# Window and rotary attention with feed-forward on one core: row-strip products split into 32-column squares, part of the first softmaxes moved to ScalarE

## The chip, the cores and the metric

The kernel runs on one NeuronCore of a Trainium2 chip. The time is device time in microseconds (us), taken over whole executions; a separate execution was recorded by the hardware profiler. TensorE (PE) multiplies into PSUM, VectorE (DVE), ScalarE (ACT) and GpSimd (POOL) do the elementwise work, SyncE (SP) issues most transfers.

## What is computed

Sixteen sequences of 512 tokens with 256 channels pass through four blocks, each added to its input:

```python
x = x + window_attention(layernorm(x))   # stage a
x = x + ffn(layernorm(x))                # stage f
x = x + rotary_attention(layernorm(x))   # stage b
x = x + ffn(layernorm(x))                # stage h, same weights as f
```

All is float32. Both attentions have 16 heads of 16 channels. Stage a is a softmax over a window of 32 keys to each side and the first 4 keys; the first 4 queries see all keys. Stage b divides exponentials of rotated scores by the sum of exponentials of unrotated ones, and masks causally after that:

```python
num = exp(q_rot @ k_rot.T * scale)
den = exp(q @ k.T * scale).sum(-1, keepdims=True)
y = where(causal, num / den, 0) @ v
ffn(x) = (silu(x @ wg.T) * (x @ wu.T)) @ wd.T      # 256 -> 768 -> 256, integer weights times 1/127
```

## The kernel before

One program holds all 16 sequences. A planner inside the kernel (`Plan`, from L85) writes out the order of every engine's instructions by hand. Each piece of work is an `Op` (L57) with an engine, an estimated duration, names that it needs, slots that it takes and gives, and for TensorE a "lying": how the 128 x 128 array is divided.

- `ROWS`: four strips of 32 rows. A head pair holds 32 channels of the contraction, so four head pairs are multiplied side by side, each into its own PSUM bank. `nm` (L1219, rotated scores) and `dn` (L1153, unrotated scores) take 128 weight columns, `sa` (L730, window scores) takes 64, with the two halves of a tile of 128 queries beside each other.
- `COLS`: four strips of 32 columns, with all 128 rows: the products of weights with values (`ya` L894, `yb` L1279) and, when the neighbours lie so, the projections (`product`, L440).
- `FULL`: the whole array: transposes (`tp` L838, `lt` L503, `tg` L964, `pgp` L866) and projections. `FLEX` work takes `FULL` after `FULL` and `COLS` otherwise.

The planner picks among the ready ops of an engine. For TensorE it adds to an op's progress an amount from `TURN` where the array would have to be divided anew, keeps row work together for `TURN["hold"]`, and counts `BORDER` for a change. `LEAD` and `SHARE` say how far the stages of one sequence run apart; all four stages of neighbouring sequences are interleaved. These numbers order the work; they are not measured times.

Stage a of a sequence projects keys, queries and values, then for each of four tiles of 128 queries computes `sa` into four banks, adds the mask into a score buffer `sc` (two of them) and runs a softmax over two halves of the heads: maximum on VectorE (L773), subtraction on POOL (L775), one exponential over 1056 columns on ScalarE (L782), sum and reciprocal on VectorE (L784, L785), scaling on POOL (L790). Then `tp` transposes the weights four heads at a time, and the results `pt` are copied out of PSUM, alternately by VectorE (L843) and ScalarE (L845). Stage b runs 16 `dn` groups of four products of 512 columns, each followed by four exponentials with a running sum on ScalarE (L1134), and 10 `nm` groups in whose causal part the columns are 512, 384 + 128 or 256 + 256, each followed by four exponentials (L1185) and a causal selection on POOL (L1195).

The first two sequences' stage a stands alone at the start, since nothing else is ready. The buffer `ht` holds the integers of `wd` until they are scaled, and later the hidden layer of a feed-forward.

Of the kernel before, what the change touches and what calls it, by code (L numbers as in the profile page):

```python
# [15 lines left out]
P = 128  # L16
S = 512
# [39 lines left out]
class Op:  # L57
# [1 line left out]


    def __init__(
        self, engine, us, *needs, takes=(), gives=(), makes=None, lying=FULL, sbuf=False
    ):
        self.engine, self.us, self.needs = engine, us, needs
        self.takes, self.gives, self.makes, self.lying = takes, gives, makes, lying
        self.sbuf = sbuf
        self.end, self.k = 0.0, {}

def pe(us, *needs, **how):
# [9 lines left out]
    return Op("pool", us or 0.15 + 0.0017 * n, *needs, **how)  # L79

LAG = {"pe": 0.26, "act": 0.2, "dve": 0.2, "pool": 0.2, "sp": 0.1}
BORDER = 0.19
NEVER = 1e9

class Plan:  # L85
# [68 lines left out]
    def run(self):  # L154
        while True:
            self.threads = [t for t in self.threads if t[1] is not None]
            if not self.threads:
                return
            cand = []
            for t in self.threads:  # L160
                op = t[1]
                at = self.ready(op)
                if at >= NEVER:
                    continue
                start = max(at, self.free[op.engine])
                if op.engine == "pe" and at > self.free["pe"]:
                    start += 0.1
                if op.sbuf:
                    start = max(start, self.sbuf)
                cand.append((start, t))  # L170
            assert cand, [(t[2], t[3], t[1].needs, t[1].takes) for t in self.threads]
            least, t = min(cand, key=lambda c: c[0])
            engine = t[1].engine
            soon = [
                c
                for c in cand
                if c[1][1].engine == engine
                and c[0]
                <= least + (TURN["hold"] if engine == "pe" and self.lying == ROWS == c[1][1].lying else 0.05)
            ]  # L180
            if engine == "pe":
                start, t = min(
                    soon,
                    key=lambda c: (
                        c[1][4],
                        self.progress(c[1]) + self.turn(c[1][1]),
                    ),
                )
            else:
                start, t = min(soon, key=lambda c: (not c[1][1].gives, c[1][4], self.progress(c[1])))  # L190
            op = t[1]
            us = op.us
            if engine == "pe":
                op.lying = self.lies(op)
                if op.lying != self.lying:
                    us += BORDER
                self.lying = op.lying

                if start - self.free[engine] > 1.5:
                    self.slow = start + 4.2  # L200
                if start < self.slow:
                    us += min(us, (self.slow - start) / 2)
                key = t[2], t[3]
                self.done[key] = self.done.get(key, 0.0) + us
            if op.sbuf:
                self.sbuf = start + us
            self.take(op)
            self.free[engine] = start + us
            op.end = start + us + LAG[engine]
            self.give(op, op.end)  # L210
            if op.makes:
                self.at[op.makes] = op.end
            try:
                t[1] = t[0].send(op)
            except StopIteration:
                t[1] = None


TURN = {"hold": 0.35, "fr": 0.05, "fc": 0.3, "rf": 0.02, "cf": 1.0, "rc": 0.05, "cr": 0.1}
LEAD = {"a": 0.0, "f": 1.015, "b": 1.665, "h": 2.889}  # L220
SHARE = {"a": 44.0, "f": 33.0, "b": 66.0, "h": 33.0}

@with_exitstack
def kernel(
# [152 lines left out]
    def dequantized():  # L377

        for at, t, raw, by, name in (
            (15.0, wg_sb, raw_wg, DEQUANT, "wg"),  # L380
            (17.0, wu_sb, raw_wu, DEQUANT, "wu"),
            (19.0, wd_sb, raw_wd, 0.5 * DEQUANT, "wd"),
        ):
            yield dve(0, at, us=0.9, makes=name, sbuf=True)
            nc.vector.tensor_scalar(t, raw, by, None, ALU.mult)
        yield dve(0, 25.0, us=1.0, makes="sins", sbuf=True)
        nc.vector.tensor_reduce(sign, perm, AX.X, ALU.add, negate=True)
# [2 lines left out]
    def values_bias():  # L390
# [3 lines left out]
        for kc in range(NC):  # L394
# [27 lines left out]
            "va": 1,  # L422
            "vw": 1,
            "sg": 1,
            "small": 2,
            "pq": 2,
            "gs": 1,
            "yg": 1,
# [4 lines left out]
            "ht": 1,  # L433
        }
    )
    x_slot = {}
    xnt = {}
    before = {"f": "a", "b": "f", "h": "b"}
# [2 lines left out]
    def product(out, w, moving, lying, **how):  # L441

        strips = [slice(32 * j, 32 * j + 32) for j in range(4)] if lying == COLS else [slice(P)]
        for s in strips:
            nc.tensor.matmul(out[s], w[:, s], moving, skip_group_check=True, **how)  # L445

    def one(op, emit):
        emit((yield op))
# [158 lines left out]
    def window_attention(b):  # L607
# [62 lines left out]
        for oc in range(NC):  # L670
# [12 lines left out]
            takes=("u", "sg"),  # L683
            gives=[("tmp", q_slot[oc]) for oc in range(NC)],
            lying=FLEX,
        )
        sgp = bank(op, [P, NT, H * NG], f"sgp_{b}")
        for t in range(NT):
# [23 lines left out]
        for t in range(NT):  # L712
# [2 lines left out]
                f"qa_{me}.0",  # L715
                f"qa_{me}.1",
                f"scored_a{b - 1}",
                takes=("s", "sc", "small"),
                makes=f"scored_{me}" if t == NT - 1 else None,
                gives=[(lock, 0) for lock in locks] if t == NT - 1 else (),  # L720
                lying=ROWS,
# [2 lines left out]
            for oc in range(NC):  # L724
                for par in range(2):
                    for half in range(2):
                        for j in range(4):
                            rows = slice(32 * j, 32 * j + 32)
                            u = 2 * t + half
                            nc.tensor.matmul(  # L730
                                ps[j][U * half : U * half + U, oc, par, :],
                                tiles["qa"][rows, par, oc, u * U : (u + 1) * U],
                                keys[rows, oc, u * U : u * U + P],
                                start=True,
                                stop=True,
                            )
            go(softmax(b, t, op, ps, sg), -1 if t < 2 else 0)

    kept = {}

    def softmax(b, t, op, ps, sg):


        me = f"a{b}"
        mask = mask3[:, 0 if t == 0 else 2 if t == NT - 1 else 1, :]
        sc = buf(op, "sc", [P, 4, NC, 2, P + NG], f"sc_{b}_{t}")
        small = buf(op, "small", [P, 2, H], f"sm_{b}_{t}")
        flat = sc.rearrange("p j c two w -> p (j c two) w")
        kept[b, t] = sc, small, op.k["sc"], op.k["small"]
        k_s, at = op.k["s"], op.end  # L750
        op = yield dve(
            0, at, f"sg_{me}", us=0.17, gives=(("sg", 0),) if t == NT - 1 else (), sbuf=True
# [17 lines left out]
        def half(hs, start, name):  # L770
            part = flat[:, hs, :]
            op = yield dve(0, *start, us=1.17)
            nc.vector.tensor_reduce(small[:, 0, hs], part, AX.X, ALU.max, negate=True)  # L773
            op = yield pool(0, op.end, us=1.9, sbuf=True)
            nc.gpsimd.tensor_tensor(  # L775
                part,
                part,
                small[:, 0, hs].unsqueeze(2).to_broadcast([P, H // 2, P + NG]),
                ALU.add,
            )  # L780
            op = yield act(1056, op.end)
            nc.scalar.activation(part, part, AF.Exp, scale=SCALE)  # L782
            op = yield dve(0, op.end, us=1.17 + 0.15)
            nc.vector.tensor_reduce(small[:, 1, hs], part, AX.X, ALU.add)  # L784
            nc.vector.reciprocal(small[:, 1, hs], small[:, 1, hs])  # L785
            op = yield pool(0, op.end, us=1.9, makes=f"sc_{me}.{t}.{name}", sbuf=True)
            if name:
# [12 lines left out]
    def global_values(b, v_all):  # L800

        me = f"a{b}"
        op = yield pe(0.43, f"v_{me}.0", takes=("u",), lying=FLEX)
        vg_ps = bank(op, [P, S], f"vgp_{b}")
        product(
            vg_ps[:, :D], spread, v_all[:, 0, :, 0::2, :], op.lying, start=True, stop=True
# [6 lines left out]
    def weighted(b):  # L813
# [10 lines left out]
        def read(t):  # L824

            left[t] = left.get(t, len(parts) + 1) - 1
            return (("sc", kept[b, t][2]),) if left[t] == 0 else ()

        def turns():
            for t in range(NT):  # L830
                for n, (oc, par) in enumerate(parts):
# [5 lines left out]
                    for j in range(4):  # L837
                        nc.tensor.transpose(ps[:, j, :], sc[:, j, oc, par, 0:P], ident)  # L838

                    def keep(_, t=t, n=n, par=par, ps=ps, op=op):  # L840
                        pt = buf(op, "pt", [P, 4, P], f"pt_{b}_{t}_{n}")
                        if par:
                            nc.vector.tensor_copy(pt, ps)  # L843
                        else:
                            nc.scalar.copy(pt, ps)  # L845
                        pts[t, n] = pt, op.k["pt"]

                    how = dict(gives=(("u", op.k["u"]),), makes=f"pt_{me}.{t}.{n}")
                    go(one(dve(S, op.end, **how) if par else act(S, op.end, **how), keep), -1)

        def weights(t):

# [20 lines left out]
        for t in range(NT):  # L873
            go(weights(t))
            for ns in (range(4),):
                op = yield pe(
                    0.22 * len(ns),
                    *(f"pt_{me}.{t}.{n}" for n in ns),
                    f"vw_{me}",
                    takes=("u",) if 0 in ns else (),  # L880
# [51 lines left out]
    def global_queries(b, qg, keys, v_all, v_lock):  # L932

        me = f"a{b}"
        R = H * NG
        op = yield pe(0.9, takes=("u", "gs"), lying=COLS)
        ps = bank(op, [P, S], f"gq_{b}")
        for oc in range(NC):
            nc.tensor.matmul(
# [106 lines left out]
    def rotary_attention(b):  # L1046
# [91 lines left out]
        for oc in range(NC):  # L1138
            for par in range(2):
                for t in range(NT):  # L1140
# [9 lines left out]
                    ps = banks(op, [P, S], f"dn_{b}_{oc}_{par}_{t}")  # L1150
                    for j in range(4):
                        rows = slice(32 * j, 32 * j + 32)
                        nc.tensor.matmul(  # L1153
                            ps[j],
                            tiles["qb"][rows, par, oc, t * P : (t + 1) * P],
                            tiles["kt"][rows, oc, :],
                            start=True,
                            stop=True,
                        )
                    go(exponentials(oc, par, t, ps, op.k["s"], op.end, last))  # L1160

# [44 lines left out]
        for i, (oc, segments) in enumerate(groups):  # L1206
# [9 lines left out]
            for c, par, at in segments:  # L1216
                n = S - c * P
                for j, rows in enumerate(strips):
                    nc.tensor.matmul(  # L1219
                        ps[j][:, at : at + n],  # L1220
                        tiles["kr"][rows, oc, c * P : (c + 1) * P],
                        tiles["qr"][rows, par, oc, c * P :],
                        start=True,
                        stop=True,
                    )
            go(causal(i, segments, ps, op), -1)

# [31 lines left out]
    def products(b, groups, made, strips):  # L1259
        me = f"b{b}"  # L1260
        seen = set()
        for i, (oc, segments) in enumerate(groups):
            first = i % (len(groups) // NC) == 0
            last = (i + 1) % (len(groups) // NC) == 0
            op = yield pe(0.8, f"num_{me}.{i}", takes=("u",) if first else (), lying=COLS)
            if first:
                seen = set()
                k_u = op.k["u"]
# [178 lines left out]
```

## Time and profile before

| | us |
|---|---|
| median of 3 runs | 2588.65 (2588.26 to 2593.74) |
| profiled execution | 2590.7 |
| its span | 2589.0 |
| TensorE busy | 2531.6, 98% |
| VectorE, ScalarE, POOL busy | 1578.8, 1456.5, 949.7 |
| `dn`, one matmul record (2048, four at a time) | 0.636 |
| `nm`, one record of 512 columns (512) | 0.632 |
| `sa`, one record (4096, eight at a time) | 0.284 |

A float32 product is carried out in two passes, and each pass is one record of a weight load (PEld) and one of a matmul (PE); transposes take one pass. Records of strips that run side by side overlap, so a record's duration says little about throughput; the distance from one group's start to the next one's does. The mean granted clock of TensorE over the execution is 0.99 of full speed.

### The profile page before, as it was taken

To read this page: it belongs to the slowest core of one execution; us is meant where nothing else is said; L and a number is where in the kernel's file an instruction comes from. 1 tells how busy PE (TensorE), PEld (TensorE's weight loads), DVE (VectorE), ACT (ScalarE), POOL (GpSimd) and SP (SyncE) were. 2 spreads that over 40 slices of the span, in tenths; PEclk is the share of its full clock that TensorE was granted. 3 is DMA by queue.
4 is the path that set the end of the run, shared out by engine and by line. 5 is a ranking of instruction groups with operands and counts; after the bars stand their busy time and mean duration, and the time that the engine had idled before them with its cause. 6 is when DMAs were issued, how large, how long until landed. Compare 5 with 4: busy or idle time off the path is not lost.

```text
span 2589.0 us, 78357 instructions
## 1 busy us (share of the span) xinstructions
PE 2531.6 (98%) x34688; PEld 1286.3 (50%) x34688; DVE 1578.8 (61%) x3062; ACT 1456.5 (56%) x3553; POOL 949.7 (37%) x971
## 2 busy tenths in 40 slices
PE   7899999999999999999999999999999999999998
PEld 5454445454454544545455454544545455454444
DVE  7975748476583755847467484665837558374332
ACT  2356664745547465474755647465474754647473
POOL 5634425153251524425153250533515144151211
PEclk8999999999999999999999999999999999999999
DMA  4000010000101000010000100000010000100000
GB/s 140 26 25 2 2 41 2 25 18 10 33 2 28 15 25 18 2 41 2 25 18 2 41 2 25 19 21 21 2 34 9 25 18 2 33 2 1 10 9 9
DMA packets 26675, 50.76 MB, mean 20 GB/s; under 512 B 2336, under 2 KB 21216, under 8 KB 26336
## 3 DMA queue, kind: packets, MB, share of 16 engines
q1 hardware_dynamic: 24976, 44.83, 6.1%
q8 instruction: 272, 4.46, 0.7%
q10 hardware_dynamic: 1360, 0.93, 0.1%
q14 instruction: 67, 0.55, 0.1%
HBM read 13.77 MB, written 8.39 MB: 9 GB/s over the span
## 4 chain that ended last, share of the span: by engine, by line
PE 85%; DVE 12%; ACT 1%; DMA 1%; POOL 1%; issue 1%; POOLq 0%; DVEq 0%; ACTq 0%
PE dn L1153 9%; PE psc_uh L445 7%; PE psc_gh L445 7%; PE nm L1219 7%; PE po_h L445 7%; PE psc_gf L445 7%; PE psc_uf L445 6%; PE po_f L445 6%; PE yb L1279 5%; PE tp L838 3%; PE sa L730 3%; PE psv_a L445 2%; PE po_b L445 2%; PE psc_qa L445 2%; PE ya L894 2%; DVE tmpb L1064 2%
## 5 line engine op out<-in xcount | busy, mean ns | idle before, releaser
L1134 ACT ACTIVATE dn<-dn 128x512 f32<-128x512 f32 x1024 | 599.4, 585 | 121.0 <-PE dn L1153 118.0
L1185 ACT ACTIVATE ptb<-nm 128x512 f32<-128x512 f32 x640 | 328.8, 610 | 241.1 <-PE nm L1219 240.8
L1195 POOL TENSOR_SCALAR_AFFINE_SELECT ptb<-ptb 128x512 f32<-128x512 f32 x256 | 160.5, 637 | 537.0 <-ACT ptb L1185 521.1
L775 POOL TENSOR_TENSOR sc<-sc,sm 128x1056 f32<-128x1056 f32 x128 | 248.8, 1951 | 258.1 <-DVE sm L773 250.2
L1153 PE MATMUL dn<-kt,qb 32*128 32x512 f32 x2048 | 295.8, 636 | 0.4 <-DVE vb L572 0.4
L790 POOL TENSOR_TENSOR sc<-sc,sm 128x1056 f32<-128x1056 f32 x128 | 249.8, 1952 | 49.9 <-DVE sm L785 34.4
L445 PE MATMUL psc_uh<-xnt_h,wu_sb 128*32 128x512 f32 (+1 forms) x1164 | 184.4, 598 | 10.7 <-DVE pt L843 10.7
L1134 ACT ACTIVATION_READ_ACCUMULATOR dn<-dn 128x1 f32 x1024 | 192.0, 188 | 0.0
L445 PE MATMUL psc_gh<-xnt_h,wg_sb 128*32 128x512 f32 (+1 forms) x972 | 190.1, 598 | 0.8 <-DVE xnt_h L511 0.8
L784 DVE TENSOR_REDUCE sm<-sc 128x8 f32<-128x1056 f32 x128 | 159.3, 1244 | 44.5 <-ACT sc L782 43.4
L1219 PE MATMUL nm<-qr,kr 32*128 32x512 f32 (+3 forms) x2048 | 186.1, 459 | 0.0
L445 PE MATMUL psc_gf<-xnt_f,wg_sb 128*32 128x512 f32 (+1 forms) x1344 | 183.0, 594 | 0.1
L445 PE MATMUL psc_uf<-xnt_f,wu_sb 128*32 128x512 f32 (+1 forms) x1368 | 182.9, 594 | 0.0
L760 DVE TENSOR_TENSOR sc<-sa,mask 128x512 f32<-128x512 f32 x256 | 161.8, 681 | 27.4 <-PE sa L730 27.3
L445 PE MATMUL po_h<-wd_sb,ht_h 128*32 128x256 f32 (+1 forms) x2496 | 177.6, 380 | 0.0
L445 PE MATMUL po_f<-wd_sb,ht_f 128*32 128x256 f32 (+1 forms) x2568 | 177.4, 379 | 0.0
L1279 PE MATMUL yb<-ptb,vb 128*32 128x512 f32 (+3 forms) x2048 | 167.1, 437 | 1.5 <-POOL ptb L1195 1.5
L1153 PEld LDWEIGHTS dn<-kt,qb 32*128 32x128 f32 x2048 | 90.7, 183 | 147.9 <-ACT dn L1134 73.5
L782 ACT ACTIVATE sc<-sc 128x1056 f32<-128x1056 f32 x128 | 138.5, 1098 | 33.5 <-POOL sc L775 32.5
L773 DVE TENSOR_REDUCE sm<-sc 128x8 f32<-128x1056 f32 x128 | 156.6, 1238 | 0.0
L445 PEld LDWEIGHTS po_h<-wd_sb,ht_h 128*32 128x32 f32 (+1 forms) x2496 | 106.8, 116 | 79.7 <-ACT xnt_f L513 9.9
L838 PE MATMUL tp<-ident,sc 128*128 128x128 f32 x1024 | 135.8, 282 | 10.1 <-POOL sc L790 10.1
(172 smaller groups left out, 3892.8 us busy)
## 6 DMA issues: line engine op xcount, KB each, us to landing
vw<-va SPq DMA_DIRECT2D x30, 576.0 KB, 5.5
x<-in_x_dram SPq DMA_DIRECT2D x16, 512.0 KB, 3.9
out_dram<-x SPq DMA_DIRECT2D x16, 512.0 KB, 2.9
vw<-va SPq DMA_DIRECT2D x30, 144.0 KB, 5.4
vw<-vb SPq DMA_DIRECT2D x2, 576.0 KB, 6.0
raw_wg_sb<-in_w_gate_dram SPq DMA_DIRECT2D x1, 768.0 KB, 9.7
raw_wu_sb<-in_w_up_dram SPq DMA_DIRECT2D x1, 768.0 KB, 11.2
raw_wd_sb<-in_w_down_dram SPq DMA_DIRECT2D x1, 768.0 KB, 12.6
```

The lines of the kernel that those rows point to most:

```text
L445: nc.tensor.matmul(out[s], w[:, s], moving, skip_group_check=True, **how)
L760: nc.vector.tensor_tensor(flat[:, 4 * j : 4 * j + 4, 0:P], ps[j].rearrange("p c two w -> p (c two) w"), mask.unsqueeze(1).to_broadcast([P, ...
L775: nc.gpsimd.tensor_tensor(part, part, small[:, 0, hs].unsqueeze(2).to_broadcast([P, H // 2, P + NG]), ALU.add,)
L784: nc.vector.tensor_reduce(small[:, 1, hs], part, AX.X, ALU.add)
L790: nc.gpsimd.tensor_tensor(part, part, small[:, 1, hs].unsqueeze(2).to_broadcast([P, H // 2, P + NG]), ALU.mult,)
L838: nc.tensor.transpose(ps[:, j, :], sc[:, j, oc, par, 0:P], ident)
L1134: nc.scalar.activation(ps[j], ps[j], AF.Exp, scale=SCALE, accum_out=den[:, t, h : h + 1])
L1153: nc.tensor.matmul(ps[j], tiles["qb"][rows, par, oc, t * P : (t + 1) * P], tiles["kt"][rows, oc, :], start=True, stop=True,)
L1185: nc.scalar.activation(pt[:, j, :], ps[j], AF.Exp, scale=SCALE)
L1195: nc.gpsimd.affine_select(out=pt[:, :, at : at + P], in_=pt[:, :, at : at + P], pattern=[[0, 4], [1, P]], compare_op=ALU.is_ge, fill=0.0, ...
L1219: nc.tensor.matmul(ps[j][:, at : at + n], tiles["kr"][rows, oc, c * P : (c + 1) * P], tiles["qr"][rows, par, oc, c * P :], start=True, sto ...
L1279: nc.tensor.matmul(y_ps[rows, c * P :], vb[:, c, 4 * oc + j, par : par + 2, :], pt[:, j, at : at + n], start=len(seen) == 1, stop=len(seen ...
```

## The change

Every row-strip product is split by a new helper, `scores`, into products of 32 weight columns. With four row strips and four column strips 16 products of 32 x 32 can be in the array at once. `sa`, `dn` and `nm` use it.

For the first two sequences, the first half of each softmax leaves POOL and VectorE: the maximum is scaled on VectorE and handed as a bias to eight ScalarE exponentials, one for each head, which also give the sums. Those sequences' `pt` are all copied by ScalarE. A third score buffer for them lies in the memory of `ht`, and a third small buffer is added.

The planner's numbers for switching (`BORDER` by pair of divisions, `TURN`), for the lead of the stages and for some durations change, so the whole order of the four stages is written anew.

```diff
-BORDER = 0.19
+BORDER = {"fr": 0.22, "fc": 0.15, "rf": 0.21, "rc": 0.13, "cf": 0.21, "cr": 0.13}
...
+                if op.lying == COLS and op.cols:
+                    us = op.cols
                 if op.lying != self.lying:
-                    us += BORDER
+                    us += BORDER[self.lying[0] + op.lying[0]]
...
-TURN = {"hold": 0.35, "fr": 0.05, "fc": 0.3, "rf": 0.02, "cf": 1.0, "rc": 0.05, "cr": 0.1}
-LEAD = {"a": 0.0, "f": 1.015, "b": 1.665, "h": 2.889}
+TURN = {"hold": 0.15, "fr": 0.15, "fc": 0.3, "rf": 1.0, "cf": 1.0, "rc": 0.2, "cr": 0.02}
+LEAD = {"a": 0.0, "f": 1.062, "b": 1.779, "h": 3.366}
...
-            yield dve(0, at, us=0.9, makes=name, sbuf=True)
+            op = yield dve(0, at, us=0.9, makes=name, sbuf=True)
+            if name == "wd":
+                plan.slots["ht"] = [op.end]
...
-            "small": 2,
+            "small": 3,
...
+    plan.slots["ht"] = [NEVER]
...
+    def scores(out, w, moving):
+
+        for i in range(0, w.shape[1], 32):
+            nc.tensor.matmul(out[i : i + 32], w[:, i : i + 32], moving, start=True, stop=True)
...
-                            nc.tensor.matmul(
+                            scores(
                                 ps[j][U * half : U * half + U, oc, par, :],
                                 tiles["qa"][rows, par, oc, u * U : (u + 1) * U],
                                 keys[rows, oc, u * U : u * U + P],
-                                start=True,
-                                stop=True,
                             )
...
+    def scores_in(b, t):
+
+        return "ht" if b < 2 and (NT * b + t) % 3 == 2 else "sc"
...
+            if b < 2 and name == 0:
+
+                op = yield dve(8, op.end)
+                nc.vector.tensor_scalar(small[:, 0, hs], small[:, 0, hs], SCALE, None, ALU.mult)
+                op = yield act(0, op.end, us=3.0)
+                for i in range(hs.start, hs.stop):
+                    nc.scalar.activation(
+                        flat[:, i, :],
+                        flat[:, i, :],
+                        AF.Exp,
+                        bias=small[:, 0, i : i + 1],
+                        scale=SCALE,
+                        accum_out=small[:, 1, i : i + 1],
+                    )
+                op = yield dve(8, op.end)
+            else:
...
-                        if par:
+                        if on_dve:
                             nc.vector.tensor_copy(pt, ps)
                         else:
                             nc.scalar.copy(pt, ps)
...
-                        nc.tensor.matmul(
+                        scores(
                             ps[j],
                             tiles["qb"][rows, par, oc, t * P : (t + 1) * P],
                             tiles["kt"][rows, oc, :],
-                            start=True,
-                            stop=True,
                         )
...
-                    nc.tensor.matmul(
+                    scores(
                         ps[j][:, at : at + n],
                         tiles["kr"][rows, oc, c * P : (c + 1) * P],
                         tiles["qr"][rows, par, oc, c * P :],
-                        start=True,
-                        stop=True,
                     )
```

Here `on_dve` is `par and b > 1`. Left out are changed estimates for single ops (`sgp`, `vgp`, `gq`, `ya`, `yb`) and the bookkeeping of the score slot.

## The prediction

> **What bounds the kernel now.** I read the head of the page first, then TensorE in order of time, then single tiles, then narrow stretches of time.
>
> ```profile
> span 2589.0 us, 78357 instructions
> PE 2531.6 (98%) x34688; PEld 1286.3 (50%) x34688; DVE 1578.8 (61%) x3062; ACT 1456.5 (56%) x3553; POOL 949.7 (37%) x971
> ...
> PE   7899999999999999999999999999999999999998
> ...
> PEclk8999999999999999999999999999999999999999
> ```
>
> TensorE (PE) is full from the third slice on at full clock. All its waits after 135 us add up to 22.9 us. So a nanosecond added to or taken from PE's own sequence is one of the span, except in the first 109 us, where VectorE leads:
>
> ```profile
> 34.00:109.00 75.00, 58.31 (x1474) 42.61 (x1473) 72.08 (x132) 26.44 (x43) 52.47 (x44) 0.86 0.11 29
> ```
>
> (columns: PE, PEld, DVE, ACT, POOL, clock: DVE 72.1 of 75 us, PE 58.3.) Next, what one group of row-strip products costs, from start to start:
>
> ```profile
> 1255.77 1.14 PE L1153 MATMUL dn<-kt,qb 32*128 32x512 f32 x8
> 1256.84 1.92 PE L445 MATMUL psc_qa<-xnt_a,wq_sb 128*32 128x512 f32 x16
> ...
> 1249.62 2.17 PE L1153 MATMUL dn<-kt,qb 32*128 32x512 f32 x16
> 1251.72 1.10 PE L894 MATMUL ya<-pt,vw 128*32 128x64 f32 x64
> ...
> 1200.05 1.21 PE L730 MATMUL sa<-kp,qa 32*64 32x128 f32 x64
> 1201.19 1.10 PE L894 MATMUL ya<-pt,vw 128*32 128x64 f32 x64
> ...
> 1282.14 0.46 PE L964 MATMUL tg<-ident,gp 64*128 64x64 f32 x4
> 1282.54 0.70 PE L445 MATMUL psc_gh<-xnt_h,wg_sb 128*128 128x512 f32 x1
> ```
>
> A product is two records (two passes; 512 columns stream in 0.427 us a pass). The dn group takes 1.07 us: 0.854 of streaming and 0.216 of switching. The parts of that are in the durations (shortest/median/longest, ns):
>
> ```profile
> L1153 PE MATMUL dn<-kt,qb x2048: 587/588/692, 166.8 to 2512.6; 32*128 32x512 f32 x187
> L730 PE MATMUL sa<-kp,qa x4096: 267/268/472, 34.1 to 2297.0; 32*64 32x128 f32 x196
> L894 PE MATMUL ya<-pt,vw x4096: 216/219/317, 60.3 to 2345.2; 128*32 128x64 f32 x196
> ```
>
> A first product after a switch lasts 692 instead of 587 ns with 128 weight columns; in the record starts of the sa and ya groups above the first ones last 318 instead of 267 (64 columns) and 243 instead of 219 (32). So the exposed weight load is 105, 51 and 25 ns. Strips start 6.7 ns apart, and 90 to 96 ns pass from the end of the last stream to the first start in the other form. dn: 105 + 3 x 6.7 + 854 + 90 = 1069 ns. This closes, so I use it below.
>
> The last view counts records begun since a group's start, on the weight-load side for sa and on the matmul side for og (the 4-column products, L984):
>
> ```profile
> 1200.00:1200.45 0.45, 0.40 (x33) 1.00 0.00 0
> 1200.00:1200.51 0.51, 0.46 (x33) 1.00 0.00 0
> 1200.00:1200.63 0.63, 0.58 (x45) 1.00 0.00 0
> ...
> 1288.40:1288.71 0.31, 0.26 (x32) 1.00 0.00 0
> 1288.40:1288.96 0.56, 0.51 (x62) 1.00 0.00 0
> 1288.40:1289.21 0.81, 0.76 (x92) 1.00 0.00 0
> ```
>
> sa begins 16 products (32 loads) and one load of a 17th, then stands still until 0.03 us after its first product has ended, though other strips are free by then. og begins 16 products in 0.26 us, then 15 in each 0.25 us, 16.7 ns each. I read: 17 products are in PE's queue at most; a place is free again only when a product has ended (its stream plus 0.16 us), and refilling takes 0.03 us, then 16.7 ns a product. With these figures sa works out at 1139 ns (shown: 1.14 us), a dn double at 1932 (least of 21: 1929), an nm pair at 1079 (measured 1079).
>
> **The change: squares.** dn, nm and sa become 32 x 32 products: dn and nm from 1024 to 4096 each, sa from 2048 to 4096; the built order has 26819 products instead of 18240. The streaming of a group stays: 4 strips of 128 columns filled the array as 16 squares do. A group of 16 squares costs 25 (load) + 15 x 6.7 (starts) + 854 + 90 = 1070 ns: 80 ns saved on the load, 80 lost on the starts. The Trainium skill, "TensorE: Matmul & The Clock Gate", Part 3, Packing small matmuls, gives about 4 ns from tile to tile; by that a group gains 40 ns, 18 us over 440 entries (an estimate from the page). I keep 6.7, which 4 and 8 strips show here.
>
> 16 squares use up the queue, so any second round waits for the first to end. Working through the same places, a square group costs:
> - dn double: 2.28 us, was 1.93
> - nm pair of 384 + 128 or 256 + 256 columns: 1.43, was 1.08
> - sa (4 rounds): 1.84, was 1.14; two in a row: 3.51, was 2.03
>
> The same page's table gives TensorE a queue of 64 and does not say what fills a place. If it is a program's load or matmul, 32 products fit; then doubles and pairs cost nothing more and sa 1.27 us, about 6 us in all, and the change comes out near 2587. The row shows 17 products, so a product fills four places, a load and a matmul for each pass; I go by the row. It speaks against this change.
>
> Counts of groups in the two built orders, before -> after: dn single 211 -> 210, double 21 -> 21; nm pairs 93 -> 94, single 36 -> 57, double 12 -> 1; sa alone 62 -> 42, two in a row 1 -> 11.
> - dn: 266.3 -> 273.6, +7.3 us
> - nm: 162.1 -> 198.0, +35.9
> - sa: 72.7 -> 115.9, +43.2, less 5.6 for the 8 of the first two sequences, beside a full VectorE: +37.6
>
> **Switches.** Entries into row or square form stay at 440. Entries into columns go from 374 to 450 (0.14 each: 25 + 20 + 95 ns), +10.6; into the full array from rows or columns from 141 to 104 (105 + 90), -7.2. Sum +3.4. One price is not in the trace: columns to squares, 396 times, where only the row size changes. Bounds 0 to 95 ns. Two near rows differ: from 64 x 128 to 128 x 128 (tg, above) 99 ns pass; from 128 x 128 to 128 x 64 only 2. The first changes rows as here, so I take 95, nothing gained; the other end is -38 us.
>
> **Start.** For one half of each of 8 score tiles a POOL addition (L775, 1.96 us), a wide exponential (L782, 1.08) and a VectorE sum (L784, 1.24) become one small VectorE product (0.2, as L785) and 8 exponentials of 132 columns. From 1056 columns in 1.08 and 512 in 0.61 (L1185) one takes 0.28, and up to 0.47 with its accumulator read (0.19, L1134); I take 0.37, 3.0 for eight. 4.3 us of chain become 3.2. 16 copies pt (L843, 0.67) go from VectorE to ScalarE. In the window above VectorE loses 6 x 1.04 + 10 x 0.67 = 13 us; ScalarE rises from 26 to 44; PE, with longer sa, to 62.5 of 75 us, which is the next limit. At most 12.5 us come off; I take 10 (4 to 13). The exponentials stand ahead of the pt copies in ScalarE's order, and transposes behind them wait for PSUM; this is why not all of it comes. The third score buffer (the memory of ht) and the third small one cost nothing while feed-forward 0 waits for attention 0 anyway; without that cover its first ht waits for tile 1 of sequence 1, some us once. SP's transfers stay at the same number, and POOL's queue only loses work.
>
> **New order in the middle.** TURN, LEAD and BORDER only choose the order; no time is taken from them. Of the 22.9 us of waits a PE that is 3% later should meet fewer: -5 (0 to -15). dn doubles partly wait already (median 2.10, not 1.93): -3.5.
>
> Sum: 7.3 + 35.9 + 37.6 + 3.4 - 10 - 5 - 3.5 = +66 us. The profiled execution took 2590.7 us (1.7 beside its span), so 2656.7; it stands 2.05 above the median of the runs, 2588.65, so **2655**.
>
> **The rivals.**
> 1. *The queue binds, but columns to squares does not drain.* 2655 - 38 = 2617. For it: the 2 ns row. Against: every change of the row size in the trace drains; the Trainium skill, "TensorEngine Tiling (Array Packing)", Key Properties, says that every change of the tiling mode drains, which the 2 ns row contradicts.
> 2. *Faster: squares stream without a queue limit and are entered without a drain.* 2588.65 + 3.4 - 37.6 - 10 = 2544. It decides if two rounds of squares follow at streaming pace (sa under 1.2 us) and the switch is below 50 ns. For it: each square has its own load, and nothing in the trace has 16 tiles. Against: 17 products at 4 and at 8 tiles alike.
> 3. *No queue limit, all switches drain.* 2588.65 + 3.4 - 10 = 2582, just beyond measuring.
> 4. *16 streams disturb each other.* dn, nm and sa stream 410 us; a quarter more is 2750 with the rest. Nothing in the trace speaks for it: 4 column strips read as much.
>
> **Numbers.** Forecast 0.45 (2635 to 2680 by its terms), rival 1 0.23, rival 2 0.20, rival 3 0.06, rival 4 0.06. 0.2% (5 us) is about what can be told from no change. Faster: 0.20 and half of rival 3, 0.23; same 0.03; slower 0.74. The range 2545 to 2685 leaves out rival 4, half of rival 2 and some tails, 0.2.
>
> **What would show it.** Right: dn, nm and sa groups at 1.07, 1.43 and 1.84 us from start to start; first products of squares lasting 25 ns more than later ones; 16 starts over 0.1 us. Wrong: an sa group near 1.1 us (the queue), columns to dn in under 1.0 us (the drain), first feed-forward products not before about 99 us (the start). Dense work after 135 us with PE below 95% would mean that the new order made waits.

## The result, and the profile after

The changed kernel takes 2726.47 us (median of 4 runs, 2721.9 to 2726.95) against 2588.45 us (2587.95 to 2593.74): 1.0528 times as long, 95% interval 1.0515 to 1.0541. The forecast was 2655, with a range of 2545 to 2685. The direction was right; the loss was twice as large, 138 us instead of 66.

The profiled execution took 2721.9 us. The head of its page:

```profile
span 2720.2 us, 113663 instructions
...
PE 2642.8 (97%) x51846; PEld 1295.2 (48%) x51846; DVE 1581.7 (58%) x3046; ACT 1483.7 (55%) x3689; POOL 956.4 (35%) x963
...
PE   7999999999999999999999999999999999999998
...
PEclk9999999999999999999999999999999999999999
...
q8 instruction: 406, 6.65, 1.0%
```

TensorE is as full as before and at full clock, but for 131 us longer. The last line is a DMA queue that the prediction never looked at: the one that brings instructions (packets, MB, share of time). The page of before has there:

```profile
q8 instruction: 272, 4.46, 0.7%
```

PE's records, loads and matmuls together, are 103,692; 6.65 MB over them is 64 bytes a record, so one packet of 16 KB holds about 256 records, or 64 float32 products of four records each (two of the expectations below speak of 128 products a portion; by this it is 64). That will matter below.

Groups in order of time on TensorE, from the changed kernel's timeline (start, duration, matmul records; a group's cost is read from its start to the next one's):

```profile
1253.16 1.16 PE L456 MATMUL nm<-qr,kr 32*32 32x512 f32 x32
1254.24 1.92 PE L451 MATMUL psc_uf<-xnt_f,wu_sb 128*32 128x512 f32 x16
1256.10 1.50 PE L456 MATMUL nm<-qr,kr 32*32 32x384 f32 x64
1257.53 1.97 PE L869 MATMUL tp<-ident,sc 128*128 128x128 f32 x16
...
1260.53 1.91 PE L456 MATMUL sa<-kp,qa 32*32 32x128 f32 x128
1262.36 1.07 PE L1308 MATMUL yb<-ptb,vb 128*32 128x384 f32 x16
```

An nm single takes 1.08 us, an nm pair 1.43, an sa group alone 1.83. The prediction had 1.07, 1.43 and 1.84. A dn single has a median of 1.087 and a dn double 2.356:

```profile
1196.87 2.42 PE L456 MATMUL dn<-kt,qb 32*32 32x512 f32 x64
1199.23 0.94 PE L1017 MATMUL og<-pgq,va 128*32 128x4 f32 x92
```

So the prices of single groups were right to a few hundredths of a microsecond. What is new is seen where two sa groups follow each other, or a group of short products follows one. The last column is idle time before the row and what ended it; "issue" is a wait that nothing in the trace released:

```profile
1041.71 3.10 PE L456 MATMUL sa<-kp,qa 32*32 32x128 f32 x217
1046.36 0.86 PE L456 MATMUL sa<-kp,qa 32*32 32x128 f32 x39 [1.55 <-issue]
1047.14 1.07 PE L1308 MATMUL yb<-ptb,vb 128*32 128x512 f32 x8
...
1263.25 0.51 PE L927 MATMUL ya<-pt,vw 128*32 128x64 f32 x23
1264.15 0.78 PE L927 MATMUL ya<-pt,vw 128*32 128x64 f32 x41 [0.39 <-issue]
```

The pair takes 5.43 us (median of the ten after 135 us: 5.09) where the forecast had 3.51. In the middle of a group, with nothing in the trace left to wait for, PE stops. All such waits after 135 us, from the waits of the changed kernel on TensorE (sum, times, longest):

```profile
PE sa L456 <- issue: 12.4, 11, 1.6
...
PE ya L927 <- issue: 5.0, 7, 1.3
PE po_h L451 <- issue: 4.0, 4, 1.5
...
PE ya L451 <- issue: 1.7, 3, 0.8
PE og L1017 <- issue: 1.7, 2, 1.1
PE nm L456 <- issue: 1.6, 4, 0.7
```

With the smaller rows they are 29 us; the kernel before has none on PE. Its other waits after 135 us, for engines and DMAs, are 23 us before and 19 after. What PE and the DMA engines do during the pair above (columns: PE, PEld, DVE, ACT, POOL, clock, DMA share, GB/s):

```profile
1041.70:1043.90 2.20, 2.20 (x171) 2.08 (x172) 0.87 (x3) 0.00 (x0) 0.10 (x1) 1.00 0.04 7
1043.90:1044.80 0.90, 0.90 (x70) 0.68 (x54) 0.90 (x3) 0.00 (x0) 0.00 (x0) 1.00 0.00 0
1044.80:1046.30 1.50, 0.01 (x1) 0.00 (x0) 1.34 (x4) 0.00 (x0) 0.00 (x0) 1.00 0.00 0
```

In these 4.6 us the only transfer is one packet of 16 KB on the instruction queue, which begins at 1043.79 us. PE runs on, loads no further weights after 1044.8, and resumes at 1046.36, 2.6 us after the packet began.

The traces of all twelve kernels measured here settle what such a wait is for. Count PE's loads, matmuls and semaphore instructions in order of start, 256 to a page; each kernel then has as many pages as packets on this queue. Every issue wait on PE, 142 in all and 119 of them after 135 us, stands at the same place of the count, 192 or 193 beyond a multiple of 256: there a page ends. Each of the 119 ends 2.2 to 3.0 us after the packet for the next page began, and of all 3739 pages that PE enters after 135 us it enters none sooner than 2.16 us after its packet began. So PE waits for its instructions.

The packet of the next page began late in these cases: from 0.8 us before to 1.9 us after PE entered the page before it (median 0.8 after). With the median of 2.4 us from packet to first use that makes about 3.2 us for a page; PE uses up a page of squares in less. What makes a packet begin when it does is not shown. No two began closer than 3.2 us in any kernel, but at the waits they were 3.4 to 19.5 us apart, so this spacing alone is not the cause.

### The profile page after: what moved, and what is told of

The parts are those of the page before. It is cut to its first block, busy times and chain, and to the rows that moved or that the text cites. A ratio compares the mean times of both kernels' runs of the same rounds, so it can differ in the third digit from the quotient of the medians.

```text
span 2720.2 us, 113663 instructions
## 1 busy us (share of the span) xinstructions
PE 2642.8 (97%) x51846; PEld 1295.2 (48%) x51846; DVE 1581.7 (58%) x3046; ACT 1483.7 (55%) x3689; POOL 956.4 (35%) x963
## 3 DMA queue, kind: packets, MB, share of 16 engines
q8 instruction: 406, 6.65, 1.0%
## 4 chain that ended last, share of the span: by engine, by line
PE 90%; DVE 6%; issue 2%; DMA 1%; ACT 1%; POOL 0%; SPq 0%; POOLq 0%; ACTq 0%; DVEq 0%
PE dn L456 10%; PE nm L456 8%; PE psc_uh L451 6%; PE po_h L451 6%; PE psc_gf L451 6%; PE psc_gh L451 6%; PE po_f L451 6%; PE psc_uf L451 6%; PE yb L1308 5%; PE sa L456 4%; PE tp L869 4%; PE ya L927 2%; PE po_b L451 2%; PE psc_qa L451 2%; PE psc_qb L451 2%; PE psv_a L451 2%
## 5 line engine op out<-in xcount | busy, mean ns | idle before, releaser
L806 POOL TENSOR_TENSOR sc<-sc,sm 128x1056 f32<-128x1056 f32 x120 | 234.4, 1957 | 270.4 <-DVE sm L788 244.8
L456 PE MATMUL dn<-kt,qb 32*32 32x512 f32 x8192 | 309.0, 600 | 3.2 <-DVE pg L903 1.6
L821 POOL TENSOR_TENSOR sc<-sc,sm 128x1056 f32<-128x1056 f32 x128 | 248.8, 1950 | 99.2 <-DVE sm L816 62.8
L456 PE MATMUL nm<-qr,kr 32*32 32x512 f32 (+2 forms) x8192 | 227.1, 441 | 1.7 <-issue 1.6
L813 ACT ACTIVATE sc<-sc 128x1056 f32<-128x1056 f32 x120 | 131.4, 1099 | 109.4 <-POOL sc L806 109.2
L1049 DVE SCALAR_TENSOR_TENSOR th_h<-th_h,psc_gh 128x512 f32<-128x512 f32 x96 | 65.9, 687 | 208.5 <-ACT th_h L1047 208.5
L451 PE MATMUL po_f<-wd_sb,ht_f 128*32 128x256 f32 x3072 | 178.1, 380 | 0.6 <-issue 0.6
L815 DVE TENSOR_REDUCE sm<-sc 128x8 f32<-128x1056 f32 x120 | 148.7, 1239 | 25.9 <-ACT sc L813 25.7
L456 PEld LDWEIGHTS dn<-kt,qb 32*32 32x32 f32 x8192 | 74.9, 103 | 177.3 <-ACT dn L1167 65.7
L456 PEld LDWEIGHTS nm<-qr,kr 32*32 32x32 f32 x8192 | 97.5, 103 | 123.6 <-issue 69.3
L606 POOL COPY rdcb<-rden 128x1024 f32<-128x1024 f32 x16 | 16.6, 1038 | 395.2 <-DVE rden L1263 390.9
```

Source lines behind the costliest of these rows:

```text
L456: nc.tensor.matmul(out[i : i + 32], w[:, i : i + 32], moving, start=True, stop=True)
L806: nc.gpsimd.tensor_tensor(part, part, small[:, 0, hs].unsqueeze(2).to_broadcast([P, H // 2, P + NG]), ALU.add,)
L821: nc.gpsimd.tensor_tensor(part, part, small[:, 1, hs].unsqueeze(2).to_broadcast([P, H // 2, P + NG]), ALU.mult,)
```

## The experiments

My theory after the result had three parts: the queue sets the prices of single groups (as predicted); the instructions of squares, used up faster than they are fetched, make the issue waits ("fetch theory" below); and the start brings nothing. Rivals were that the new order, and not the squares, costs the time; that squares disturb each other's streams; and that the number of instructions as such slows PE down. The intervals of sa_only, nm_only and dn_only rest on two runs each and are wider.

| kernel | us | against before |
|---|---|---|
| strips_new_order | 2593.35 | 1.0017 (1.0010 to 1.0023) |
| halves | 2588.82 | 0.9998 (0.9989 to 1.0007) |
| sa_only | 2662.64 | 1.0288 (1.0267 to 1.0308) |
| nm_only | 2632.32 | 1.0170 (1.0150 to 1.0191) |
| dn_only | 2612.93 | 1.0094 (1.0074 to 1.0114) |
| squares_old_order | 2700.6 | 1.0435 (1.0418 to 1.0453) |
| softmax_only | 2589.64 | 1.0001 (0.9992 to 1.0009) |
| halves_old_order | 2579.74 | 0.9962 (0.9949 to 0.9975) |
| sa_spaced | 2650.24 | 1.0237 (1.0219 to 1.0255) |
| more_products | 2607.52 | 1.0073 (1.0056 to 1.0090) |

**One product kind at a time.** Five kernels are the changed kernel, with its order and softmax, and differ only in the weight columns that `scores` takes at a time:

```diff
-    def scores(out, w, moving):
-        for i in range(0, w.shape[1], 32):
-            nc.tensor.matmul(out[i : i + 32], w[:, i : i + 32], moving, start=True, stop=True)
+    def scores(out, w, moving, cols):
+        for i in range(0, w.shape[1], cols):
+            nc.tensor.matmul(out[i : i + cols], w[:, i : i + cols], moving, start=True, stop=True)
...
```

| | sa | dn | nm |
|---|---|---|---|
| strips_new_order (as before the change) | 64 | 128 | 128 |
| halves | 64 | 64 | 64 |
| sa_only | 32 | 128 | 128 |
| nm_only | 64 | 128 | 32 |
| dn_only | 64 | 32 | 128 |

strips_new_order, expected:

> The changed kernel with dn, nm and sa back in strips (128 and 64 weight columns); its order of work and its softmax stay. Theory (queue: 17 products are in TensorE's queue and a place is free only when a product has ended, so a second round of 16 squares waits): groups return to 1.07 us (dn), 1.08 (nm pair), 1.14 (sa), and the time to 2580 to 2592 us; the waits marked issue go too. Rival (the new order costs): it stays above 2650.

Measured: 2593.35, 4.5 us more than before, just above the range expected. So the new order with the new softmax costs 0.17%, and the squares all the rest, 133 us (129.8 between the profiled executions). Attributed by group, from start to start for the groups after 135 us in both traces: sa +55.8, nm +40.4, dn +14.9, ya +9.3, and 9 in small pieces, the first 135 us among them. Two sa groups in a row take 2.094 us here, and of issue waits after 135 us these are left:

```profile
PE po_h L451 <- issue: 4.4, 5, 1.8
PE og L1018 <- issue: 0.2, 1, 0.2
```

They were expected to go altogether, and did not: the new order brings 4.6 us of them without any square, in po_h right after the short products of og. The rival "the order" falls as the cause of the loss.

sa_only, expected:

> Only sa in squares, dn and nm in strips, order and softmax of the changed kernel. Queue theory: 1.84 us a group where it stands alone, and with the waits marked issue beside sa and the ya after it, 55 to 65 us above the strips run. Rival (the waits marked issue come from all squares together): sa pairs near 3.5 us and ya without such waits, 43 us above.

Measured: 69 us above strips_new_order, 4 more than expected. An sa group alone takes 1.831 us, two in a row 5.08. By group (after 135 us, here and below): sa +54.2, ya +10.8. The waits show what comes on top:

```profile
PE sa L456 <- issue: 10.3, 8, 1.6
PE ya L928 <- issue: 7.2, 9, 1.4
```

ya is unchanged, and yet it waits. Its 64 matmul records pass in 0.92 us, and in all nine cases an sa group stands right before it or with one yb group between. Two of the nine, from the timeline:

```profile
759.64 1.90 PE L456 MATMUL sa<-kp,qa 32*32 32x128 f32 x128
761.47 0.65 PE L928 MATMUL ya<-pt,vw 128*32 128x64 f32 x31
763.38 0.69 PE L928 MATMUL ya<-pt,vw 128*32 128x64 f32 x33 [1.27 <-issue]
...
1720.18 1.90 PE L456 MATMUL sa<-kp,qa 32*32 32x128 f32 x128
1722.01 1.07 PE L1311 MATMUL yb<-ptb,vb 128*32 128x384 f32 x16
1722.90 0.40 PE L928 MATMUL ya<-pt,vw 128*32 128x64 f32 x15
1723.75 0.89 PE L928 MATMUL ya<-pt,vw 128*32 128x64 f32 x49 [0.46 <-issue]
```

Without the yb group, which passes few records in its 0.89 us, the wait of these two is longer by about as much. One line of the same trace also shows the exposed load (shortest/median/longest duration of an sa record, ns):

```profile
L456 PE MATMUL sa<-kp,qa x8192: 264/268/293, 31.4 to 2390.9; 32*32 32x128 f32 x200
```

The longest is 25 ns over the median, as predicted for 32 columns.

nm_only, expected:

> Only nm in squares, dn and sa in strips, order and softmax of the changed kernel. Queue theory: pairs 1.43 us, singles 1.08, 34 to 42 us above the strips run, nearly no waits marked issue. Rival (16 streams disturb each other): singles of 512 columns would be longer than 1.1 us as well.

Measured: +39 us over strips_new_order. Pairs take 1.425, singles 1.087, and the issue waits after 135 us stay nearly those of strips_new_order (po_h 6.0, nm 0.7). An nm pair passes 64 matmul records in 1.43 us, 45 in a microsecond where sa and ya pass 70; it pays for the queue and hardly for the fetch.

dn_only, expected:

> Only dn in squares, nm and sa in strips, order and softmax of the changed kernel. Queue theory: singles 1.09, doubles 2.36 us, 12 to 15 us above the strips run with few issue waits. Rival (16 streams disturb each other): more than 20 us. With sa (69) and nm (39) the three parts should add up to the 133 us between the changed kernel and its strips run, so some 25 if they share nothing.

Measured: +19.6 us over strips_new_order, with dn +13.9, og +2.5 and ya +2.0; somewhat more than expected. The three parts give 69 + 39 + 20 = 128 of the 133, so they nearly add up.

halves, expected:

> dn and nm in products of 64 weight columns, 8 at a time; sa in strips of 64 as before; order and softmax of the changed kernel. Queue theory: two rounds of 8 fit into 17 places, so dn doubles and nm pairs cost nothing more (1.9 and 1.05 us), and a single group gets cheaper, 51 + 7 x 6.7 + 854 + 90 = 1042 instead of 1070 ns; about 10 us below the strips run of the same order. Rival (more and smaller tiles are slower in themselves): between the strips run and the changed kernel, nm pairs near 1.25.

Measured: 4.5 us under strips_new_order. dn singles take 1.044, doubles 1.902, nm pairs 1.049, where the queue's prices gave 1.042 for a single: half the load is exposed, and eight products leave places in the queue free for the next round. The groups gain what the prices say; the kernel gains half of it.

**The squares in the old order.** The kernel before, with `scores` for 32 columns put into sa, dn and nm, and nothing else changed, so that every group stands where it stood:

```diff
+    def scores(out, w, moving):
+        for i in range(0, w.shape[1], 32):
+            nc.tensor.matmul(out[i : i + 32], w[:, i : i + 32], moving, start=True, stop=True)
...
-                            nc.tensor.matmul(
+                            scores(
...
```

> The kernel before with dn, nm and sa in squares; its order of work and its softmax stay, so that sa groups stand alone (62 alone, one two in a row). Queue theory: sa +45, nm +38, dn +9, ya behind sa +5, together some 97 us, about 2686, if the waits marked issue belong to sa groups two in a row (fetch theory: TensorE's instructions arrive 128 products at a time, and two sa groups use up one portion sooner than the next is there). Rival (the issue waits come with the number of instructions, wherever they stand): as far above before as the changed kernel is above its strips run, 133 us, 2722.

Measured: 2700.6, +112 us. sa +40.0, nm +39.2 and dn +6.8 make 86, where the prices gave 92; og +9.5, lt_f +4.2, the feed-forward projections +7.5 and ya +2.6 are the rest. Its order has a single pair of sa groups, and there is no issue wait in sa after 135 us. Those that are left lie in groups of short products:

```profile
PE og L987 <- issue: 5.5, 5, 1.3
...
PE lt_f L508 <- issue: 1.8, 3, 0.9
PE ya L897 <- issue: 1.4, 1, 1.4
```

The loss lies between the two expectations: the prices alone were too little, the full loss of the changed kernel too much. Over the kernel with strips in the same order the squares cost 21 us less here than in the changed kernel, and 16 of the 21 are in sa, whose groups do not stand in a row here.

**Spacing the sa groups.** sa_only, with the planner told to leave 4 us between a sequence's sa groups:

```diff
+        spaced = 0.0
         for t in range(NT):
             op = yield pe(
                 1.0,
+                spaced,
...
+            spaced = op.end + 4.0
```

> The run with only sa in squares, with the planner kept from putting one sa group within 4 us of another of the same sequence, so that all 64 stand alone; the order around them shifts with that. Fetch theory: the ten groups two in a row at 5.1 us become twenty of 1.83, 14 us less than that run, and no issue waits within sa. Rival (5.1 us is the queue's alone): no difference, and sa above 1.83 at other places.

Measured: 12.4 us less than sa_only, with the same products (the four runs spread over 11 us, from 2646.0 to 2657.1). All 64 sa groups now stand alone, at a median of 1.832 us:

```profile
PE ya L931 <- issue: 4.0, 5, 1.4
...
PE ya L451 <- issue: 1.3, 1, 1.3
...
PE sa L456 <- issue: 0.6, 1, 0.6
```

10.3 us of issue waits in sa become 0.6. So the wait depends on how closely the products follow each other.

**As many products, spread out.** The kernel before, with every gate, up, query and key projection in column form cut into four products of 128 columns: nearly as many PE records (101,920) and instruction packets as the changed kernel, but evenly spread.

```diff
+        n = S // 4 if op.lying == COLS else S
+        for at in range(0, S, n):
             for kc in range(NC):
                 product(
-                    ps,
+                    ps[:, at : at + n],
...
-                    x_in[:, kc, :],
+                    x_in[:, kc, at : at + n],
```

> The kernel before, strips and order untouched, with each projection in column form (gate, up, query, key) in four products of 128 moving columns instead of one of 512: 26376 products, as many as with all squares (26432), at 54 ns each and never more than 4 tiles. Fetch theory in its burst form (issue waits come only where 128 products pass in under some 3.5 us): no issue waits; 12 more gaps of 2.3 ns a group for 339 groups, 9 us more, 2598. Rival (waits come with the number of instructions): issue waits of 10 us or more on top, 2608 to 2630.

Measured: +19 us where 9 were expected. Its queue and the longest of its issue waits after 135 us:

```profile
q8 instruction: 399, 6.54, 1.0%
```

```profile
PE psc_gf L445 <- issue: 1.1, 2, 0.7
```

399 packets and only 1.5 us of such waits: the number of instructions does not make them. A projection here passes 64 matmul records and as many loads in some 1.75 us, so 256 records of them last 3.5 us, more than the 3.2 us worked out above for a page. An sa group has 256 records with its loads, as many as one packet, and is gone in 1.83. The loss lies in the projections (17 us), which have three more seams in each stream. Seams at the price expected are 9 us of it; the other 8 I can't account for.

**The softmax alone.** The kernel before with the softmax, `pt`, and buffer parts of the change, row strips and the old ordering numbers:

```diff
+            if b < 2 and name == 0:
...
+                op = yield act(0, op.end, us=3.0)
+                for i in range(hs.start, hs.stop):
...
-                        if par:
+                        if on_dve:
...
```

> The kernel before with the softmax parts of the change alone: half of the first two sequences' softmax on ScalarE, their pt copies on ScalarE, third score and small buffers; strips, and the planner's numbers of before. Forecast of the prediction for this part: 10 us less (4 to 13), 2579. What the trace of the changed kernel suggests (TensorE has done the same work only 2 us earlier at 100 us): 0 to 3 us less.

Measured: 2589.64, no difference. The start did change, as the windows of its trace show (PE, PEld, DVE, ACT, POOL, clock, DMA share, GB/s):

```profile
34.00:109.00 75.00, 61.68 (x1521) 41.49 (x1509) 65.93 (x135) 44.33 (x146) 44.63 (x41) 0.88 0.11 28
```

Against the window of before VectorE lost 6 us and POOL 8, ScalarE gained 18. At 155 us PE was some 3 us ahead of before in streaming done; by 278 us the lead was gone. The waits of its TensorE from 0 to 280 us show a part of that:

```profile
PE lt_a L514 <- DVE xn_a L486: 11.2, 2, 9.6
...
PE sgp L451 <- issue: 2.3, 1, 2.3
PE tp L869 <- POOL sc L821: 2.2, 2, 1.2
PE nm L456 <- DVE sc L775: 2.1, 1, 2.1
```

and of before:

```profile
PE lt_a L503 <- DVE xn_a L475: 9.6, 1, 9.6
PE tp L838 <- POOL sc L790: 8.3, 5, 3.7
```

Of tp's wait for POOL 6.1 us went; but lt_a waits 1.6 us longer, and the waits of sgp (for instructions, by its place in a page) and nm, 4.4 together, were not there. The order is another, too. Which of these takes the rest isn't separated.

**The version that the runs pointed to.** The kernel before, with dn and nm in products of 64 columns; sa has 64 already:

```diff
+    def scores(out, w, moving):
+        for i in range(0, w.shape[1], 64):
+            nc.tensor.matmul(out[i : i + 64], w[:, i : i + 64], moving, start=True, stop=True)
...
```

> The kernel before with dn and nm in products of 64 weight columns, sa in strips of 64 as it was; order and softmax of before. Queue theory: singles 1.044 instead of 1.071 us (247), pairs 1.049 instead of 1.077 (93), doubles 1.902 instead of 1.929 (33): 10 us less, 2579, if no wait takes it back. Rival (the 27 ns a group are taken back by waits for the exponentials): the same as before.

Measured: 2579.74, 0.9962 of before (0.9949 to 0.9975), 9 us less; dn -6.5 and nm -4.4 by group. It beats both kernels. A dn group costs 1.04 us from start to start:

```profile
1251.38 1.11 PE L450 MATMUL dn<-kt,qb 32*64 32x512 f32 x16
1252.42 1.92 PE L445 MATMUL psc_qa<-xnt_a,wq_sb 128*32 128x512 f32 x16
```

## Where the prediction was wrong, and what of it held

Its sum against the runs, profiled executions (2721.9 - 2590.7 = 131.2 us). The measured rows of dn, nm and sa are the changed kernel less strips_new_order, groups after 135 us:

| step | forecast, us | measured, us |
|---|---|---|
| dn | +7.3 | +14.9 |
| nm | +35.9 | +40.4 |
| sa | +37.6 | +55.8 |
| ya and all other groups | 0 | +18.7 |
| switches, start, waits in the middle, dn waits | 3.4 - 10 - 5 - 3.5 = -15.1 | +1.4 (strips_new_order less before; +4.5 by the medians) |
| sum | +66 | +131 |

**The step that failed** is "New order in the middle": "a PE that is 3% later should meet fewer" waits, -5, with the bound 0 to -15 on one side only. For the waits that it looked at, those for other engines and DMAs, it was nearly right: 23 us after 135 us became 19. It left out that PE can also wait for its own instructions, of which the change makes 49% more (103,692 records for 69,376): 0 before, 29 us after. Most of the sa and ya rows' excess is of this kind. sa two in a row was priced at 3.51, as more rounds of the queue; it costs 5.09, which over the ten pairs after 135 us is 16 us of the 18 by which sa missed. ya was priced at nothing; sa_only alone has ya +10.8, 7.2 of it in such waits. The prediction counted the pairs (1 before, 11 after) and even priced them, but took the second as a longer first. The runs that separate this: sa_spaced (same products, waits gone from sa), more_products (nearly as many packets, 1.5 us of waits), squares_old_order (one pair of sa groups, at the start, and no waits in sa after 135 us). That the waits are for the next page of instructions is shown by their place, the same in all 142.

The Trainium skill describes this fetch ("Runtime: NRT & Kernel Launch", Instruction fetch mechanics): pages of 16 KiB, 256 instructions, the next brought while the current one runs, at a cost "mostly hidden". The size agrees with this trace's 64 bytes a record. That it stays hidden does not: 29 us of waits here, because 256 records of squares can be used up in 1.83 us while PE never entered a page sooner than 2.16 us after its fetch began. The measurement decides.

**The start** was the second step that failed: -10, measured about 0. ScalarE's time in the window from 34 to 109 us rose to 44 us as forecast, and one exponential of 132 columns took 0.39 us for 0.37; but VectorE lost 6 us of it in softmax_only and 5 in the changed kernel where 13 were forecast. What PE gained, some 3 us at 155 us, did not last. The prediction bounded the gain at 4 to 13 and so left out zero; it named only waits that would keep a part of it, not those that would come in their place.

**The queue** was the step that carried the sign, and it held: single groups at 1.83, 1.43 and 1.09 us, the three kinds apart in three kernels, and the 64-column version at 1.044, for which the same prices gave 1.042 beforehand. Rivals 2 and 3, squares that stream without a limit, are excluded by these rows; the one that was to come out faster needed an sa group under 1.2 us. Its weakest single figures are the dn double (2.356, not 2.28: 21 times 0.08, 1.6 us) and singles after columns (1.087, not 1.070; after the whole array they take 1.070). These 17 ns lie in the starts: the first and the sixteenth square start 119 ns apart after columns (7.9 ns each) and 100 ns after the whole array (6.7 each, as forecast). Why is open. The recorded dn sum also has a slip: 210 singles and 21 doubles at its own prices are 272.6, not 273.6, so its forecast was +6.3.

**The drain from columns to squares** was the one price taken between 0 and 95 ns. Counted as the prediction counts, from the end of the last stream, 395 of the 396 such switches in the changed kernel take about 95. The profile's ends of matmuls are modelled, so the surer reading is the difference: the next form starts 70 ns before the end on record of the matmul before it, where between 128 x 128 and 128 x 64 it starts 164 ns before. Rival 1 falls. Here the statement of the Trainium skill ("TensorEngine Tiling (Array Packing)", Key Properties) that a change of tiling mode drains agrees with the rows; for the change between 128 x 128 and 128 x 64 it does not.

**Rival 4**, sixteen streams that disturb each other, falls too: a dn single of sixteen squares is 16 ns longer than one of four strips, not a quarter.

So of the 65 us missed, 37 lie in sa, ya and the other groups, 16.5 in the last row of steps (about 10 of it the start), 12 in dn and nm. Issue waits beyond those of strips_new_order (29.0 less 4.6) are 24 of the 65, most of them in the 37; those 4.6 us, which the order brings by itself, are in the last row. The remainder of the 37 was not separated.

## What to carry to other kernels

Count products, not only streaming time: with 16 small products in the array, every second round waited for the first to end, so dividing dn and nm paid at 64 columns (eight products: 11 us less in these groups) and not at 32 (sixteen: 46 us more in the same order). Count instructions per microsecond where short products stand close together: in these runs PE could stop where 256 load and matmul records passed in less than about 3.2 us. It did not always: of the pages that PE used up in under 2.4 us, 69 ended in a wait and 63 did not. Those 63 had the packet of the next page begun 0.1 to 2.7 us before PE entered them. A gain at the start of a kernel is worth nothing until the wait that comes next has been named and costed.

## What the runs showed of the hardware that was not expected

- TensorE waits for its own instructions at full load: up to 1.6 us at a time, 29 us in all after 135 us, in the changed kernel. In every kernel that has such waits they stand where a page of 256 instructions ends, and after 135 us each ended 2.2 to 3.0 us after the next page's fetch began.
- Dividing rows as well as columns drains: from columns (128 x 32) to squares (32 x 32) the first start came 94 ns later, against the record before it, than between 128 x 128 and 128 x 64, and it was the same on the way back.
- Dividing a group's weights more finely helps only while the products fit in the queue: a dn single took 1.071 us with 128 columns, 1.044 with 64 and 1.087 with 32.
- Sixteen squares start 7.9 ns apart after columns and 6.7 ns apart after the whole array.
